# A GPS layer on one core: normed rows and queries issued earlier, 22 expert steps ahead, 60 posted columns, 21 diagonal tiles, statistics by algebra

## The chip, the cores and the metric

The kernel runs on one core of one Trainium2 chip. The metric is the device time of one execution in microseconds, as the median over runs. A core has five engines that run their own instruction streams and wait for each other by semaphores: TensorE (PE in the profile; its weight loads are shown as PEld), VectorE (DVE), ScalarE (ACT), GpSimd (POOL, which here issues all indirect DMAs) and SyncE (SP, which issues the plain DMAs).

## What is computed

`reference` is one layer of a graph network (GPS) over 3125 nodes with 256 features, in float32: a message-passing block and a linear-attention mixer on the normed nodes, added to the input, and then a mixture of experts with a graph-attention gate.

```
xn = _layernorm(x, axis=-1)
x = x + _L0_gnn_ref(xn, edge_attr_64, src, dst, ...) + _L0_mix_ref(xn[None], ...)[0]
x = x + _L0_ffn_ref(_layernorm(x, axis=-1)[None], ..., L0_ffn_edge_index)[0]
```

The message block gathers xn for 103125 edges sorted by target, appends 64 edge features, multiplies by a 320x256 matrix, sums by target, and runs a norm, a three-layer MLP with skips and a norm. The mixer has 4 layers. Each is

```
h = _layernorm(x, ln1_g[i], ln1_b[i])
x = x + _linear_attn(h, Wq[i], Wk[i], Wv[i], Wo[i], bo[i])
h = _layernorm(x, ln2_g[i], ln2_b[i])
x = x + (gelu(h @ W1[i] + b1[i], approximate=False) @ W2[i] + b2[i])
```

with 8 heads of 32. Queries are a softmax over the features of a head, keys a softmax over all nodes, and the context of a head is keys^T @ values. The expert block scores each node with graph attention over 65536 random edges (leaky_relu, softmax by target, sum of messages of 16 features), norms the scores, takes the best two of four experts, and adds their gated outputs; an expert is 256 to 512 to 256 with gelu.

## The kernel before

Nodes lie in 25 tiles of 128 rows (`NT`), kept in `xm` ([128, 25, 256]). `FOURS` are chunks of four tiles and a last one of one tile; `CHUNKS` is the same list with the one-tile chunk in sixth place, ahead of the last four tiles; `PAIRS` are chunks of two.

**Start.** `node_norm` takes bn_stats and bn_aggr of each tile, the root and reciprocal (`rstd_of`), and norms the rows on ACT in place. The normed rows go to `xn_d`. Then a flag (`unsorted`) is loaded into registers, which opens a branch for unsorted targets that is not taken. After it the statistics of the normed rows are taken again for the mixer (L330-331).

**Messages.** Edges are laid out 806 columns by 128. For each column POOL gathers 128 rows of `xn_d` (L515), in three rotating buffers `m_run` of 8 columns, and DVE adds a running sum over a partition's edges (L527), which is written to `run_d`. These sums are placed in DVE's order by a planner: every piece of the mixer calls `pace(us)`, which moves a clock and emits the columns that are due by it (one per 1.27 us). `beside(us)` spends idle time on a list of jobs that count, sort and place the 65536 gate edges.

**Mixer.** First the keys of layer 0 for all chunks. Then for each layer: `combined` makes `co` (the context with the output matrix), and each chunk goes through `attend` (add to `xm`, statistics), `normed_T` to `h2`, `ff_up` (8 blocks of matmuls and gelu), and `ff_down`. Behind it by one chunk run the next layer's `norm1` (in the middle of `ff_up`), `keys` (at its end; `query` is called at the end of `keys`) and `context` (after `ff_down`). The matmul outputs of `keys`, `query`, `attend`, `ff_up` and `ff_down` share three PSUM buffers named ps_a; a buffer is taken again once its last reader is done. In `keys` the two halves are both held until their exp, which needs the maximum over both (`top`).

**Placing the gate edges.** Jobs compute the sorted place of each edge. For 32 columns of 128 edges at a time (`SG`) the tile `place` is written by DVE (L691), and each column is then sent to `by_dst` by one indirect DMA on POOL (L856), except the first `SENT_BY_PE` = 3 of each group but the last: these are posted by a one-hot matmul on PE (`post`, L844-846) into one PSUM tile, which `sorted_edges` reads at the end. So 45 columns are posted and 467 sent. Message gathers and sends stand in one queue on POOL.

**Gate.** `finish` norms the final rows, writes a table of 24 features a node, and scatters the target's term to `tgt_d` on POOL (L917). Edges are then worked in 16 chunks of about 26 columns: POOL gathers 21 rows of the table for each (L1356), and 5 more are made by PE with a one-hot matrix (`which`, L1342, made from `low_of`, which `turned` transposes and writes through DRAM, L1329). Each `edge_chunk` runs scans on DVE and exps on ACT.

**Experts.** The experts' work is a generator of 164 steps (`expert`): a block of matmuls and a gelu, or the output of two tiles. `advance(n)` runs it up to step n. `LEAD` = 12 steps are issued ahead of the first edge chunk, 10 of them ahead of `turned`, and the rest is spread evenly over the chunks (`EACH`). The instructions of these steps are held in program order.

**End.** POOL gathers the sums of each node (L1594), DVE makes the gates, and the gated outputs are added: for the pairs in `by_pe` (8 pairs, 16 tiles) ACT scales an identity by each gate (L1730), PE multiplies it with the expert's output (L1732, summed over the four experts in PSUM), and DVE adds the sum (L1742); for the other 9 tiles DVE adds expert by expert (`by_turns`, L1750). Each pair is stored as it is done.

Of the kernel before, what the change touches and what calls it, by code (L numbers as in the profile page):

```python
# [13 lines left out]
ALU = mybir.AluOpType  # L14
# [45 lines left out]
def kernel(ctx: ExitStack, tc: tile.TileContext, a: dict, out: bass.AP):  # L60
# [47 lines left out]
    def stats(src, mv):  # L108
        st = small.tile([P, 6], F32, name="bst")
        V.bn_stats(st, src)  # L110
        V.bn_aggr(mv, st)
# [96 lines left out]
    def node_norm(c):  # L208
        for t in c:
            stats(xm[:, t, :], mv[:, t, :])  # L210
        r = rstd_of(mv[:, c[0]:c[-1] + 1, :], eps5)
        for i, t in enumerate(c):
            normed(xm[:, t, :], xm[:, t, :], r, i)
        nc.sync.dma_start(xn_d[c[0] * P:(c[-1] + 1) * P, :].rearrange("(c p) d -> p c d", p=P),
                          xm[:, c[0]:c[-1] + 1, :])

    for c in FOURS[:4]:
        node_norm(c)
# [108 lines left out]


    first_weights = layer_weights(0)
    for t in range(NT):  # L330
        stats(xm[:, t, :], mv[:, t, :])
    nc.sync.dma_start(res_d[:P, :].rearrange("p (a b) -> p a b", b=160), zero[:, :160].rearrange("p (o c) -> p o c", o=1).to_broadcast([P, 2, 160]))
    nc.sync.dma_start(run_d[NO_SUM:NO_SUM + 1, :].rearrange("p (a b) -> p a b", b=160),
                      zero[:1, :160].rearrange("p (o c) -> p o c", o=1).to_broadcast([1, 2, 160]))
# [483 lines left out]
    SG = 4 * GC  # L818
    number = [so.tile([P, SG], F32, name=f"number{i}") for i in range(2)]

    SENT_BY_PE, MID = 3, SRC // 2 - 486
    by_pe, posted = [], []

    def sent_by_pe(t):
# [220 lines left out]
        for kc in range(2):  # L1045
            V.scalar_tensor_tensor(wv[:, kc, :], ps[:, 1, :], -1.0 / D, wv[:, kc, :], op0=ALU.mult, op1=ALU.add)

    def normed_T(c, g, b, name):
        r = rstd_of(mv[:, c[0]:c[-1] + 1, :], eps5)
        hn = []  # L1050
        for i, t in enumerate(c):
            h = mw.tile([P, D], F32, name="hn", bufs=4)
            normed(h, xm[:, t, :], r, i)
            hn.append(h)
        hx = mw.tile([P, 2, 512], F32, name=name, bufs=1)
        transposed(hx[:, :, :len(c) * P], hn, g, b)
        return hx, r

    class Keys:
        pass  # L1060
# [9 lines left out]
    def halves(c):  # L1070
        return [c[i:i + 2] for i in range(0, len(c), 2)]

    def norm1(kv, l, c):
        kv.made[c[0]] = [normed_T(c, att_w[l]["g1"], att_w[l]["b1n"], "h1")]
        pace(1.5 * len(c) / 4)

    def keys(kv, l, c):

        (h1, r), = kv.made[c[0]]
        n = min((c[-1] + 1) * P, N) - c[0] * P  # L1080
        kT = mw.tile([P, 2, 512], F32, name="kT", bufs=1)
        if n < len(c) * P:
            V.memset(kT[:, :, n:len(c) * P], 0.0)
        here = small.tile([P, 2], F32, name="here", bufs=2)
        both = []
        for m in range(2):
            ps = pa.tile([P, 512], F32, name="ps_a")
            for kc in range(2):
                T.matmul(ps[:, :n], att_w[l]["wk"][:, kc, m * P:(m + 1) * P], h1[:, kc, :n], start=kc == 0, stop=kc == 1)  # L1089
            V.tensor_reduce(here[:, m:m + 1], ps[:, :n], AX.X, ALU.max)  # L1090
            both.append(ps)
        top = small.tile([P, 2], F32, name="top", bufs=2)
        down = small.tile([P, 2], F32, name="down", bufs=2)
        if kv.top is None:
            V.tensor_scalar_mul(top, here, -QS)
        else:
            V.scalar_tensor_tensor(top, here, -QS, kv.top, op0=ALU.mult, op1=ALU.min)
            V.tensor_tensor(down, top, kv.top, op=ALU.subtract)
        add = small.tile([P, 2], F32, name="add", bufs=2)
        for m in range(2):  # L1100
            S.activation(kT[:, m, :n], both[m][:, :n], AF.Exp, bias=top[:, m:m + 1], scale=QS, accum_out=add[:, m:m + 1])  # L1101
        if kv.top is None:
            V.tensor_copy(kv.ksum, add)
        else:
            S.activation(down, down, AF.Exp)
            V.tensor_tensor(kv.ksum, kv.ksum, down, op=ALU.mult)
            V.tensor_tensor(kv.ksum, kv.ksum, add, op=ALU.add)
        first = kv.top is None
        kv.top = top
        pace(3.7 * len(c) / 4)  # L1110
        qs_of = []
        for i0, ts in enumerate(halves(c)):
            qs_of.append(query(l, ts, h1, 2 * i0 * P))
        kv.made[c[0]] = [r, kT, down, first, qs_of]

    def query(l, c, h1, o):
        k = len(c)
        ps = pa.tile([P, 2, D], F32, name="ps_a")
        for i, t in enumerate(c):
            for kc in range(2):  # L1120
                T.matmul(ps[:, i, :], h1[:, kc, o + i * P:o + (i + 1) * P], att_w[l]["wq"][:, kc, :], start=kc == 0, stop=kc == 1)  # L1121
        q = mw.tile([P, 2 * HEADS, DH], F32, name="q", bufs=3)
        nh = k * HEADS
        ps_q = ps[:, :k, :].rearrange("p t (h d) -> p (t h) d", h=HEADS)
        qm = small.tile([P, 2 * HEADS, 1], F32, name="qm")
        V.tensor_reduce(qm[:, :nh, :], ps_q, AX.X, ALU.max)
        V.tensor_tensor(q[:, :nh, :], ps_q, qm[:, :nh, :].to_broadcast([P, nh, DH]), op=ALU.subtract)
        S.activation(q[:, :nh, :], q[:, :nh, :], AF.Exp, scale=QS)
        qs = small.tile([P, 2 * HEADS, 1], F32, name="qs")
        V.tensor_reduce(qs[:, :nh, :], q[:, :nh, :], AX.X, ALU.add)  # L1130
        V.reciprocal(qs[:, :nh, :], qs[:, :nh, :])
        V.tensor_tensor(q[:, :nh, :], q[:, :nh, :], qs[:, :nh, :].to_broadcast([P, nh, DH]), op=ALU.mult)
        pace(1.9 * k / 2)
        return q
# [104 lines left out]
    for l in range(DEPTH):  # L1239
        print('K',l,round(clock['now']),clock['columns'],len(jobs),clock['sent'],len(pieces))  # L1240
        if l == 0:
            fold(0)
        co = combined(kv, l)
        held[0] = GROUPS - 5
        beside(20.0)
        if l + 1 < DEPTH:
            att_w[l + 1] = layer_weights(l + 1)
        if l:
            ff_weights(l)
        if l == 1:  # L1250
            zero_fills()
        kv = keys_begin() if l + 1 < DEPTH else None
        attend(co, CHUNKS[0])
        h2, _ = normed_T(CHUNKS[0], ff_w[l]["g2"], ff_w[l]["b2n"], "h2")
        for j, c in enumerate(CHUNKS):
            last = CHUNKS[j - 1] if j else None
            ff_up(l, c, h2, 0, 3)
            if last and kv:
                norm1(kv, l + 1, last)
            ff_up(l, c, h2, 3, FF // P)  # L1260
            if last and kv:
                keys(kv, l + 1, last)
            if last and not kv:
                waiting.append(last)
                if j == len(CHUNKS) - 1:
                    while clock["columns"] < TM or pieces:
                        pace(2.0)
                        beside(3.0)
                for _ in range(2):
                    if len(waiting) > 1 and clock["columns"] == TM and not pieces:  # L1270
                        finish(waiting.pop(0))
            if j + 1 < len(CHUNKS):
                attend(co, CHUNKS[j + 1])
            ff_down(l, c)
            if j + 1 < len(CHUNKS):
                h2, _ = normed_T(CHUNKS[j + 1], ff_w[l]["g2"], ff_w[l]["b2n"], "h2")
            if last and kv:
                context(kv, last)
            if j == 1 and kv:
                fold(l + 1)  # L1280
        if kv:
            norm1(kv, l + 1, CHUNKS[-1])
            keys(kv, l + 1, CHUNKS[-1])
            context(kv, CHUNKS[-1])
        else:
            for c in waiting:
                finish(c)
# [216 lines left out]
        ("own_bin", "lo", "base"), ("own_bin", "hi", "base"), ("own_bin", "ohT1", "base"), ("own_bin", "ohT0", "base")))]  # L1504
    work = (w for e in range(NEXP) for w in expert(e))
    STEPS = NEXP * sum(FF2 // P + len(c[::2]) for c in FOURS)
    LEAD = 12
    EACH = (STEPS - LEAD) / N_FEW
    done, bound = [0], [False]

    def advance(to):
        while done[0] < min(to, STEPS) and next(work, False):
            done[0] += 1
# [6 lines left out]

    last, taken = None, gathered(0)
    many = nc.values_load(many_i[0:1, 0:1], min_val=0, max_val=1)
    advance(LEAD - 2)
    turned()
    marked(0)
    advance(LEAD)
    between(0, taken, LEAD)
# [211 lines left out]
            nc.sync.dma_start(out[c[0] * P:N, :], xm[:LAST, c[0], :])  # L1739

    def added(c, ps):
        V.tensor_tensor(xm[:, c[0]:c[-1] + 1, :], ps, xm[:, c[0]:c[-1] + 1, :], op=ALU.add)  # L1742
        stored(c)

    def by_turns(c):
# [4 lines left out]
                V.scalar_tensor_tensor(x, y, gate[:, t, e:e + 1], x, op0=ALU.mult, op1=ALU.add)  # L1750
        stored(c)

    by_pe, by_dve = PAIRS[:8], PAIRS[8:]
    for _ in gates(0):
        pass
    laid_out = []
# [1 line left out]
    for _ in gates(1):  # L1758
        for _ in range(1):
            if len(laid_out) < 3:  # L1760
                c = by_pe[len(laid_out)]
                laid_out.append((c, by_diagonals(c)))
    n_laid = len(laid_out)
    for k, c in enumerate(by_pe):
        added(*laid_out[k])
        if n_laid < len(by_pe):
            c = by_pe[n_laid]
            laid_out.append((c, by_diagonals(c)))
            n_laid += 1
        if k >= len(by_pe) - len(by_dve):  # L1770
            by_turns(by_dve[k - len(by_pe) + len(by_dve)])


# [22 lines left out]
```

## Time and profile before

| | us |
|---|---|
| median of 3 runs | 2413.49 (2407.11 to 2422.24) |
| profiled execution | 2414.89 |
| its span on the core | 2413.0 |
| first message gather on POOL | 34.56 |
| message gathers and layers 0, 1, most of 2 | until about 1207 |
| sends, rest of layer 2, layer 3 | 1207 to 1884 |
| scatters, table | 1884 to 1907 |
| 16 edge chunks and expert steps | 1907 to 2341 |
| node sums, gates, gated outputs | 2341 to 2413 |

The profile is one execution. Busy time counts an engine's own instructions; the idle time ahead of an instruction is given with what released it. For an indirect DMA on POOL the busy time is that of making the descriptors, and "issue" is time in which POOL waited for nothing that the profile shows. "L515" is a line of the kernel, and a line can be that of a helper: L110 and L111 are the two instructions of `stats`, L118 to L124 those of `rstd_of` and `normed`, L160 and L165 those of `transposed`. PEclk is the granted TensorE clock as a share of full speed.

### The profile page before, as it was taken

The page shows a single profiled execution, that of the slowest core. Times are in us where ns is not written, and L with a number is a line of the kernel's source. Part 1 is how long each engine was busy: PE and PEld are TensorE (multiplying, and loading weights), DVE is VectorE, ACT ScalarE, POOL GpSimd, SP SyncE. Part 2 cuts the span into 40 slices and gives each one's busy share as a digit, 9 for nine tenths or more (in the row PEclk, how much of TensorE's full clock was granted, in tenths as well). Part 3 has the DMA queues.
Part 4 walks back from the last instruction along what each step waited for, and adds up shares of the span by engine and source line. Part 5 has one row for each costly group of instructions (what it writes and reads, how often), then busy time and mean ns, then how long its engine had stood idle before and what let it go on. Part 6 is the DMA issues. An engine that isn't in the chain of part 4 may idle for free. (4 is left out here: it accounts for less than half of the span.)

```text
span 2413.0 us, 32637 instructions
## 1 busy us (share of the span) xinstructions
PE 2055.1 (85%) x10120; PEld 1420.4 (59%) x10120; DVE 1531.4 (63%) x4643; ACT 1101.1 (46%) x2028; POOL 1676.7 (69%) x1696
## 2 busy tenths in 40 slices
PE   3879787768799998799988888999989499999975
PEld 2656554555556666476666556676676265565544
DVE  7877876767647756576676475665662155655556
ACT  5734335535344453435456566656664033333324
POOL 4566767767666776567777767677777777777752
PEclk9989887888999999899988998999999699999987
DMA  8987887888866887668752232332320112211112
GB/s 252 327 277 255 272 249 258 230 231 275 255 214 223 265 249 235 222 218 254 251 159 58 52 96 68 93 81 70 80 50 5 23 31 44 54 29 31 25 20 62
DMA packets 318767, 370.50 MB, mean 154 GB/s; under 512 B 183707, under 2 KB 265732, under 8 KB 305380
## 3 DMA queue, kind: packets, MB, share of 16 engines
q1 hardware_dynamic: 251508, 253.66, 33.3%
q0 software_dynamic: 67072, 114.64, 18.0%
q8 instruction: 82, 1.34, 0.2%
q14 instruction: 105, 0.86, 0.1%
HBM read 207.95 MB, written 164.28 MB: 154 GB/s over the span
## 5 line engine op out<-in xcount | busy, mean ns | idle before, releaser
L515 POOL DMA_INDIRECT m_run<-xn_d,src_i x806 | 811.1, 1006 | 390.0 <-issue 216.7
L856 POOL DMA_INDIRECT by_dst<-pairs,place x467 | 465.7, 997 | 156.6 <-issue 136.6
L527 DVE SCALAR_TENSOR_TENSOR m_run<-m_run,stay 128x320 f32<-128x320 f32 x805 | 440.2, 547 | 63.7 <-DMA m_run<-xn_d,src_i 51.0
L1209 PE MATMUL ps_a<-h,w 128*128 128x512 f32 (+1 forms) x896 | 383.4, 568 | 4.4 <-ACT h L165 3.5
L1356 POOL DMA_INDIRECT rows_c<-tab_d,si x325 | 316.3, 973 | 98.9 <-issue 96.8
L1220 PE MATMUL ps_a<-w,gT 128*128 128x256 f32 x1600 | 367.6, 383 | 0.0
L1220 PEld LDWEIGHTS ps_a<-w,gT 128*128 128x128 f32 x1600 | 302.3, 191 | 50.5 <-issue 8.1
L1209 PEld LDWEIGHTS ps_a<-h,w 128*128 128x128 f32 x896 | 161.2, 200 | 148.6 <-issue 130.4
L1210 ACT ACTIVATE gT<-ps_a,b 128x512 f32<-128x512 f32 (+1 forms) x224 | 139.9, 633 | 147.3 <-PE ps_a L1209 145.8
L124 ACT ACTIVATE hn<-xm,rstd 128x256 f32<-128x256 f32 x225 | 120.7, 593 | 62.1 <-DVE rstd L120 59.6
L1121 PE MATMUL ps_a<-wq,h 128*128 128x256 f32 x400 | 104.2, 403 | 25.7 <-ACT kT L1101 16.6
L1477 ACT ACTIVATE hf<-ps_a,be 128x512 f32<-128x512 f32 (+1 forms) x112 | 70.3, 641 | 117.1 <-PE ps_a L1473 116.6
L1147 PE MATMUL ps_g<-xm,kr 128*128 128x256 f32 x400 | 111.8, 420 | 9.6 <-ACT kr L1145 9.3
L160 PE MATMUL ps_t<-ident,hn 128*128 128x128 f32 x450 | 81.2, 312 | 42.3 <-ACT hn L124 37.5
L792 ACT ACTIVATE earlier<-ps_t,slope 128x512 f16<-128x512 f32 x128 | 93.8, 775 | 49.2 <-PE ps_t L791 48.4
L1349 DVE SCALAR_TENSOR_TENSOR ps_g<-tile_ids,high_of,ps_g 128x500 f32<-128x500 f32 x50 | 37.1, 741 | 120.7 <-PE ps_g L1347 120.7
L1491 PE MATMUL ps_t<-we2h,hf 128*128 128x256 f32 x400 | 95.9, 392 | 14.2 <-ACT hf L1477 14.1
L1121 PEld LDWEIGHTS ps_a<-wq,h 128*128 128x128 f32 x400 | 76.4, 198 | 52.0 <-ACT kT L1101 22.7
L1147 PEld LDWEIGHTS ps_g<-xm,kr 128*128 128x128 f32 x400 | 80.7, 210 | 43.8 <-ACT kr L1145 28.3
L1089 PE MATMUL ps_a<-h,wk 128*128 128x512 f32 (+1 forms) x224 | 102.7, 592 | 3.3 <-ACT h L165 2.6
L110 DVE BATCH_NORM_STATS2 bst<-xm 128x6 f32<-128x256 f32 x250 | 97.5, 408 | 6.1 <-DVEq L303 4.1
L160 PEld LDWEIGHTS ps_t<-ident,hn 128*128 128x128 f32 x450 | 55.5, 154 | 73.7 <-ACT hn L124 55.4
(455 smaller groups left out, 3837.3 us busy)
## 6 DMA issues: line engine op xcount, KB each, us to landing
run_d<-m_run SPq DMA_DIRECT2D x100, 1280.0 KB
m_run<-in_edge_attr_dram SPq DMA_DIRECT2D x95, 256.0 KB
hr<-row_h SPq DMA_DIRECT2D x64, 256.0 KB
m_run<-xn_d,src_i POOLq DMA_INDIRECT x806
w<-in_L_mix_W_dram SPq DMA_DIRECT2D x8, 1024.0 KB
by_dst<-pairs,place POOLq DMA_INDIRECT x467
rows_c<-tab_d,si POOLq DMA_INDIRECT x325
run_d<-rows_c SPq DMA_DIRECT2D x15, 312.0 KB
```

What stands on the lines that cost most here:

```text
L124: S.activation(dst, src, AF.Identity, bias=r[:, 1, i:i + 1], scale=r[:, 0, i:i + 1])
L160: T.transpose(ps[:, i * P:(i + 1) * P], src[:, c * P:(c + 1) * P], ident)
L515: last_gather[0] = G.indirect_dma_start(out=m[:, t, :D], out_offset=None, in_=xn_d, in_offset=bass.IndirectOffsetOnAxis(ap=src_i[:, t0 + t ...
L527: add = V.scalar_tensor_tensor(m[:, t, :], before_m, stay[:, c:c + 1], m[:, t, :], op0=ALU.mult, op1=ALU.add)
L856: i = G.indirect_dma_start(out=by_dst, out_offset=bass.IndirectOffsetOnAxis(ap=place[:, t:t + 1], axis=0), in_=pairs0[:, t:t + 1], in_offs ...
L1089: T.matmul(ps[:, :n], att_w[l]["wk"][:, kc, m * P:(m + 1) * P], h1[:, kc, :n], start=kc == 0, stop=kc == 1)
L1121: T.matmul(ps[:, i, :], h1[:, kc, o + i * P:o + (i + 1) * P], att_w[l]["wq"][:, kc, :], start=kc == 0, stop=kc == 1)
L1147: T.matmul(ps_x[:, m, :], kr[:, m * P:(m + 1) * P], xm[:, t, :], start=i == 0 and m == 0, stop=i == len(c) - 1, skip_group_check=True)
L1209: T.matmul(ps[:, :w], ff_w[l]["w1"][:, kc, f * P:(f + 1) * P], h2[:, kc, :w], start=kc == 0, stop=kc == 1)
L1210: S.activation(gT[:, f, :w], ps[:, :w], AF.Gelu, bias=ff_w[l]["b1"][:, f:f + 1])
L1220: T.matmul(ps[:, i, :], gT[:, f, (2 * i0 + i) * P:(2 * i0 + i + 1) * P], ff_w[l]["w2"][:, f, :], start=False, stop=f == FF // P - 1, skip_ ...
L1356: G.indirect_dma_start(out=rows_c[:, t - COLS[j], :], out_offset=None, in_=tab_d, in_offset=bass.IndirectOffsetOnAxis(ap=si[:, t:t + 1], a ...
```

## The change

Six edits, all in the order and the amount of work; the arithmetic differs in one place.

- The statistics of the normed rows are not measured again. `node_norm` multiplies each variance twice by the reciprocal root and sets the mean to zero.
- `SENT_BY_PE` goes from 3 to 4: 60 columns are posted and 452 sent.
- `normed_T` is split into `normed_rows` (root, reciprocal, rows on ACT) and `columns_of` (transposes). The rows of `norm1` are made after 2 of the 8 blocks of `ff_up` and their transposes after 5 (before: both after 3). The rows for `h2` are made before `ff_down`, their transposes after it as before.
- `query` is called at the start of `keys`, ahead of the keys' matmuls.
- `LEAD` goes from 12 to 22: 14 steps, then `turned`, 6 more, `marked(0)`, 2 more.
- `by_pe` gets three more items (21 tiles), `by_dve` keeps two pairs (4 tiles), added after the seventh and eighth item of `by_pe`.

```diff
@@ node_norm
+        var, y = mv[:, c[0]:c[-1] + 1, 1], r[:, 0, :len(c)]
+        for _ in range(2):
+            V.tensor_tensor(var, var, y, op=ALU.mult)
+        V.memset(mv[:, c[0]:c[-1] + 1, 0], 0.0)
@@
-    for t in range(NT):
-        stats(xm[:, t, :], mv[:, t, :])
@@
-    SENT_BY_PE, MID = 3, SRC // 2 - 486
+    SENT_BY_PE, MID = 4, SRC // 2 - 486
@@
-    def normed_T(c, g, b, name):
+    def normed_rows(c):
         r = rstd_of(mv[:, c[0]:c[-1] + 1, :], eps5)
...
+        return r, hn
+
+    def columns_of(c, hn, g, b, name):
         hx = mw.tile([P, 2, 512], F32, name=name, bufs=1)
         transposed(hx[:, :, :len(c) * P], hn, g, b)
-        return hx, r
+        return hx
@@ keys
         (h1, r), = kv.made[c[0]]
+        qs_of = []
+        for i0, ts in enumerate(halves(c)):
+            qs_of.append(query(l, ts, h1, 2 * i0 * P))
...
         pace(3.7 * len(c) / 4)
-        qs_of = []
-        for i0, ts in enumerate(halves(c)):
-            qs_of.append(query(l, ts, h1, 2 * i0 * P))
@@ layer loop
-            ff_up(l, c, h2, 0, 3)
+            ff_up(l, c, h2, 0, 2)
+            rows_1 = normed_rows(last) if last and kv else None
+            ff_up(l, c, h2, 2, 5)
             if last and kv:
-                norm1(kv, l + 1, last)
-            ff_up(l, c, h2, 3, FF // P)
+                norm1(kv, l + 1, last, rows_1)
+            ff_up(l, c, h2, 5, FF // P)
...
                 attend(co, CHUNKS[j + 1])
+                rows_2 = normed_rows(CHUNKS[j + 1])[1]
             ff_down(l, c)
             if j + 1 < len(CHUNKS):
-                h2, _ = normed_T(CHUNKS[j + 1], ff_w[l]["g2"], ff_w[l]["b2n"], "h2")
+                h2 = columns_of(CHUNKS[j + 1], rows_2, ff_w[l]["g2"], ff_w[l]["b2n"], "h2")
@@
-    LEAD = 12
+    LEAD = 22
@@
+    advance(LEAD - 8)
+    turned()
     advance(LEAD - 2)
-    turned()
     marked(0)
     advance(LEAD)
@@
-    by_pe, by_dve = PAIRS[:8], PAIRS[8:]
+    by_pe, after_all, by_dve = PAIRS[:8], PAIRS[8:10] + PAIRS[12:], PAIRS[10:12]
...
+    by_pe = by_pe + after_all
     for k, c in enumerate(by_pe):
         added(*laid_out[k])
...
-        if k >= len(by_pe) - len(by_dve):
-            by_turns(by_dve[k - len(by_pe) + len(by_dve)])
+        if 6 <= k < 6 + len(by_dve):
+            by_turns(by_dve[k - 6])
```

## The prediction, made before the changed kernel was run

> **What bounds the kernel now.** I read the page first (busy shares, then the costliest groups), then busy time by stage, then the waits of PE and POOL, and last the timeline of single chunks and of the tail. The profiled run took 2414.89 us around a span of 2413.0, so 1.9 us lie outside the span; it stands 1.4 us above the median of 2413.49, which is within the spread of the three runs. Sums below are made in span time and added to the median.
>
> ```profile
> PE 2055.1 (85%) x10120; PEld 1420.4 (59%) x10120; DVE 1531.4 (63%) x4643; ACT 1101.1 (46%) x2028; POOL 1676.7 (69%) x1696
> ...
> L515 POOL DMA_INDIRECT m_run<-xn_d,src_i x806 | 811.1, 1006 | 390.0 <-issue 216.7
> L856 POOL DMA_INDIRECT by_dst<-pairs,place x467 | 465.7, 997 | 156.6 <-issue 136.6
> ```
>
> POOL looks only 69% busy, but each indirect DMA carries about 0.30 us of "issue" that is not counted: 1.26 us each. Some stages (start:end, length, then busy PE, PEld, DVE, ACT and POOL, then the granted clock):
>
> ```profile
> 490.00:830.00 340.00, 290.77 (x1270) 201.62 (x1269) 226.93 (x575) 141.84 (x247) 233.19 (x236) 0.91 0.77 247
> 830.00:1207.00 377.00, 345.89 (x1371) 237.32 (x1370) 246.05 (x597) 167.39 (x291) 259.94 (x265) 0.96 0.75 239
> 1207.00:1884.00 677.00, 601.73 (x4079) 439.20 (x4078) 397.65 (x1407) 389.21 (x700) 501.78 (x502) 0.93 0.28 72
> 1910.00:2322.00 412.00, 388.38 (x1294) 240.58 (x1294) 227.10 (x793) 134.53 (x204) 313.76 (x323) 0.97 0.19 34
> ```
>
> Layers 1 and 2 (650 to about 1330) are PE's: it is 92% busy in 830:1207, and a chunk of four tiles takes 47 us there, against 37 columns x 1.26 = 46.6 us on POOL. From 1207 to 1884 POOL (502 + 502x0.30 = 652 of 677 us) and PE share the bound; POOL runs dry whenever PE and DVE are late with `place`, once for 12.7 us at 1395. From 1910 to 2322 POOL is full (314 + 323x0.30 = 411 of 412 us); the rest is a serial tail.
>
> **Query ahead of keys (the largest part).** One chunk of layer 1 before:
>
> ```profile
> 716.98 3.60 PE L1089 MATMUL ps_a<-h,wk 128*128 128x512 f32 x8
> 720.41 3.96 PE L1121 MATMUL ps_a<-wq,h 128*128 128x256 f32 x16
> 724.21 3.62 PE L1198 MATMUL ps_a<-co,hT 128*128 128x256 f32 x16
> 728.97 0.39 PE L1217 MATMUL ps_a<-b_parts,ones_b 65*128 65x512 bf16 x1 [1.15 <-DVE q L1127]
> ```
>
> From keys to the first matmul of `ff_down`: 12.0 us, with one wait of 1.15. These blocks share three ps_a buffers. In the changed kernel's instruction order PE runs query half 0, query half 1, keys 0, keys 1, attend 0, attend 1. By then both keys tiles still hold their buffers: their exp needs `top`, which needs the maximum of both. So attend 1 takes the buffer of attend 0, and waits for the DVE add into xm. In DVE's order that add stands behind the maximum of keys 0, two sums, two reciprocals and two products of the query, three message columns (L527), the maximum of keys 1, and `top`. With this timeline's starts (128x512 on DVE 0.6 to 0.7 us, reciprocal 0.16, column 0.46; PE 1.98 us a query half, 1.8 for the others): keys 0 end at 5.8, maximum to 6.6, sums to 7.8, reciprocals to 8.1, products and three columns to 10.2, maximum and the last column to 11.4, `top` 11.5, add to 12.2. PE is done with attend 0 at 9.4, so it stands still **2.9 us**; `ff_down` starts at 14.1: +2.1 us. What is late next is everything on PE; nothing hides it, because PE is the bound here.
>
> A stop of 2.9 us may also cost clock. The Trainium skill ("TensorE: Matmul & The Clock Gate", section "What's actually happening") says the clock falls to half after an idle window of about 3.4 us; by that a stop of 2.9 us is free. The trace says otherwise (a stop of 2.98 us ends at 970.4; the seventh figure is the clock):
>
> ```profile
> 963.00:967.40 4.40, 4.05 (x20) 3.07 (x18) 3.16 (x10) 1.60 (x3) 3.46 (x4) 1.00 0.73 178
> 967.40:970.40 3.00, 0.04 (x1) 0.00 (x0) 2.93 (x12) 1.35 (x4) 2.11 (x3) 0.74 1.00 342
> 970.40:974.00 3.60, 2.92 (x9) 1.66 (x10) 0.41 (x1) 2.89 (x5) 2.69 (x4) 0.50 1.06 423
> 974.00:978.00 4.00, 4.00 (x6) 1.66 (x5) 0.69 (x1) 0.00 (x0) 3.08 (x4) 0.50 0.87 267
> ```
>
> Stops of 2.55 (at 1604), 2.75 (849), 2.98 and 3.37 us (1446) were each followed by 3.4 to 8 us at 0.50 to 0.59; stops of 2.00 and 2.45 us (1372, 1780) left it at 1.00. Half speed for 3.4 to 8 us costs 1.7 to 4 us. I take the row, 2.8 us in three of four stops: 2.1 a chunk. Sum: 5 chunks x 2 layers x (2.1 + 2.1) = **+42 us**; by the page's window, +21.
> In layer 0, where POOL or DVE set the pace up to 490, I take +3 (between +15 and -12: the wait of 9.3 us of query on the keys' exp at 512.87 may go). At the three layer ends both queries now stand ahead of the keys' chain to `co`: +2.7 less the waits of 1.4 and 1.3 that vanish, so 0 to +3 each: **+4**.
>
> **Normed rows earlier.**
>
> ```profile
> PE ps_t L160 <- ACT hn L124: 37.5, 11, 5.5
> PE ps_a L1121 <- ACT kT L1101: 16.6, 6, 9.3
> ```
>
> Of these waits, 5.3 us at 663 and 4.3 at 1005 are layer starts, which stay as they are. The ones taken away are those after the one-tile chunk, 4.92 us at 583 and 5.26 at 924: `ff_down` of one tile (3.5 us) is too short to cover the chain add, statistics, root, rows. Started before `ff_down`, the chain ends about 1 us after it, and the half clock after both stops (3.4 us each by the rows there) goes too: -2 x 7.5 = **-15 us**. Elsewhere the transposes did not wait, so 0. Of the activation tables 4 loads fewer are issued: 1.28 us each by the trace, 2.66 each with the drain by the skill ("ScalarE: Activation LUTs", "What ACT_TABLE_LOAD costs"); 5 or 11 us of an engine at 46%, so 0.
>
> **Statistics by algebra.** 25 pairs of bn_stats and bn_aggr go (25 x 0.39 = 9.8 us of DVE from 33.06 on), 21 small operations of 0.1 to 0.15 come (about 2.8). DVE reaches the flag some 1.6 us later than 28.98, since digit work is now scheduled ahead of it, so POOL's first gather (34.56) slips by that; PE's first layer matmuls come about 5 us earlier. POOL is not full at this point (120 us of gaps until 1207): **-5 us** (-8 to +2).
>
> **60 posted columns.** 15 sends leave POOL: 15 x 1.26 = 18.9 us. But:
>
> ```profile
> POOL by_dst L856 <- DVE place L691: 12.7, 1, 12.7
> ```
>
> POOL had nothing queued when `place` came at 1395, 1527, 1604 and 1720; what it saves before 1720 it waits at the next `place`. Only the 4 sends after that count: -5. The 15 posts add on PE 0.38 us each and wait 0.39 each (17.7 us over 45 for `post_hot`), on DVE 0.25 + 0.41: at most +11.6, of which I take half since PE is 89% busy. **+1 us** (-19 to +7).
>
> **22 steps ahead.** 10 steps of some 1.9 us move into PE's stops of 19.2 us (low_of, until 1889.84) and 15.4 (`which`, until 1916.54). Expert 1's five weight loads now enter SP's queue ahead of the low_d store. `which` is 17 us earlier than the first 21 gathers of rows_c, so a delay there is covered. Later POOL is the bound, so steps taken out of it give 0; one step fewer lies before the last chunk's exp: **-1 us**. A low_d store late by more than those 17 us would cost.
>
> **21 diagonal tiles.** In the tail:
>
> ```profile
> 2388.27 11.78 ACT L1730 ACTIVATE diag<-ident,gate 128x128 f32<-128x128 f32 x40
> ...
> 2407.41 0.68 DVE L1742 TENSOR_TENSOR xm<-ps_a,xm 128x512 f32<-128x512 f32 x1
> ```
>
> DVE's 36 turns fall to 16 (20 x 0.39 = 8 us less), ACT's copies rise from 64 to 84 (0.295 each, ends 2406.0). But PE takes 8 matmuls x 0.216 = 1.73 us a tile without a break from 2388.7 to 2406.1: five more tiles end at 2414.7, the last add at 2415.1 instead of 2408.1: **+7 us**.
>
> Sum: 42 + 3 + 4 - 15 - 5 + 1 - 1 + 7 = +36: **2449 us**.
>
> **Rivals.**
> 1. The stop comes, the clock stays (chance 0.20): 36 - 21 = +15, 2428. For it: the page's window, and two stops near 2.4 us left no mark.
> 2. Not slower: POOL and not PE decides (0.18). Place: 1207 to 1884. If POOL keeps a backlog at each `place`, PE's stops are absorbed and all 15 sends count: -18.9 - 5 - 1 + 7 = -18, 2395; with PE's late sum kept below POOL's saving of 19 us. Against it: the empty queue at four places, and 92% PE ahead of them. With the 9.3 us of layer 0 also gone it falls below 2389.
> 3. Worse (0.12): every stop halves the clock, also four in layer 0 (+15 more), and the columns come late into DVE's row: +60, 2473.
>
> Likeliest 0.50: 2449, itself 2435 to 2465. A measurement here tells about 1% (24 us). Faster by over 1%: half of rival 2, 0.09, so 0.10 with the rest. Slower (over 2438): 0.44 of the likeliest, 0.12, and 0.04 of rival 1: 0.60; same 0.30. Range 2393 to 2474, which leaves out the far ends of rivals 2 and 3.
>
> **What would show it.** A wait of attend (`co,hT`) on DVE xm of some 3 us in each chunk, with half clock after it; the hn waits at 583 and 924 gone; POOL waiting longer for `place`; PE's diagonals ending 8 us after ACT's. Wrong if attend 1 does not wait, or if layers 1 and 2 take no longer than before.

## The result, and the profile after

The changed kernel takes 2430.96 us (median of 6 runs, 2427.71 to 2435.57), the kernel before 2414.86 in the same series: a ratio of 1.0062, with a 95% interval of 1.0044 to 1.0080. So it is slower, by some 15 us or 0.6%, where the forecast said 36. The profiled execution has a span of 2429.2 us.

The waits of PE in the changed kernel (total, times, longest):

```profile
PE ps_a L1204 <- DVE xm L1205: 31.6, 10, 6.7
...
PE ps_t L160 <- ACT hn L124: 19.4, 7, 5.0
PE ps_t L1149 <- ACT kT L1110: 18.6, 7, 5.1
...
PE ps_a L1098 <- DVE q L1133: 15.3, 6, 10.1
```

The first line is new: `attend` waits for the add into xm. The second was 37.5 us before. One chunk of layer 1 shows where (the timeline of PE, then part of DVE's):

```profile
710.40 3.62 PE L1127 MATMUL ps_a<-wq,h 128*128 128x256 f32 x16
713.85 3.60 PE L1098 MATMUL ps_a<-h,wk 128*128 128x512 f32 x8
717.28 1.89 PE L1204 MATMUL ps_a<-co,hT 128*128 128x256 f32 x8
721.88 3.10 PE L1204 MATMUL ps_a<-co,hT 128*128 128x256 f32 x8 [2.70 <-DVE xm L1205]
724.78 0.63 PE L1223 MATMUL ps_a<-b_parts,ones_b 65*128 65x512 bf16 x1
```

```profile
715.77 0.69 DVE L1099 TENSOR_REDUCE here<-ps_a 128x1 f32<-128x512 f32 x1 [0.30 <-PE ps_a L1098]
716.38 1.27 DVE L1136 TENSOR_REDUCE qs<-q 128x16 f32<-128x512 f32 x2
717.56 0.37 DVE L1137 RECIPROCAL qs<-qs 128x16 f32<-128x16 f32 x2
717.85 0.68 DVE L1138 TENSOR_TENSOR q<-q,qs 128x512 f32<-128x512 f32 x1
718.45 0.55 DVE L529 SCALAR_TENSOR_TENSOR m_run<-m_run,stay 128x320 f32<-128x320 f32 x1
718.91 0.72 DVE L1138 TENSOR_TENSOR q<-q,qs 128x512 f32<-128x512 f32 x1
719.55 0.54 DVE L529 SCALAR_TENSOR_TENSOR m_run<-m_run,stay 128x320 f32<-128x320 f32 x1
720.01 0.68 DVE L1099 TENSOR_REDUCE here<-ps_a 128x1 f32<-128x512 f32 x1
720.61 0.54 DVE L529 SCALAR_TENSOR_TENSOR m_run<-m_run,stay 128x320 f32<-128x320 f32 x1
721.07 0.16 DVE L1104 TENSOR_SCALAR top<-here 128x2 f32<-128x2 f32 x1
721.14 0.68 DVE L1205 TENSOR_TENSOR xm<-ps_a,xm 128x512 f32<-128x512 f32 x1
```

PE is done with attend 0 at 719.2 and stands until 721.88: 2.70 us, where the forecast had 2.9. The row of DVE work ahead of the add is the one that was predicted, down to the third column between the second maximum and `top`. `ff_down` starts 14.4 us after the first matmul of the block (before 12.0). The forecast had 14.1 without any loss of clock; here 1.1 us of the 14.4 is clock, since the second attend half takes 3.10 us and not 1.99. In the next chunk, which keeps its clock, the block takes 13.3 us (763.76 to 777.04). The windows after this stop, after the next one, and after a third (start:end, length, busy PE, PEld, DVE, ACT, POOL, then the clock):

```profile
721.88:725.28 3.40, 3.40 (x10) 2.55 (x11) 2.30 (x8) 2.12 (x5) 2.48 (x4) 0.61 0.36 107
725.28:728.68 3.40, 3.40 (x16) 2.92 (x15) 3.37 (x12) 0.30 (x1) 0.82 (x1) 0.89 0.68 261
775.21:778.61 3.40, 3.40 (x16) 2.91 (x17) 3.33 (x12) 2.20 (x6) 2.49 (x4) 1.00 0.38 112
824.13:827.53 3.40, 3.40 (x10) 2.60 (x11) 2.68 (x10) 2.21 (x6) 2.18 (x3) 0.63 0.93 333
```

After 721.88 the loss is 0.39 + 0.11 of 3.40 us = 1.7 us, one such window at half clock, and after 775.21, at the same length of stop (2.67 us), it is nothing. Of eight such stops between 565 and 1176, six show half clock and two do not. Of the ten chunks in layers 1 and 2, seven stop ahead of attend 1; the two ahead of a one-tile chunk, which has no attend 1, stop ahead of `ff_down` instead; one shows no such stop. The two ahead of `ff_down` keep their clock, though one is the longest stop of the nine:

```profile
874.50 0.38 PE L1223 MATMUL ps_a<-b_parts,ones_b 65*128 65x512 bf16 x1 [3.31 <-DVE xm L1205]
```

```profile
874.50:877.90 3.40, 3.40 (x16) 3.00 (x16) 2.67 (x10) 2.77 (x7) 2.79 (x3) 1.00 0.39 116
```

So five of nine stops in layers 1 and 2 cost a window.

How far the changed kernel stands behind at a few places (start of the instruction before and after, in us):

| | before | after | shift |
|---|---|---|---|
| first message gather | 34.56 | 33.5 | -1.1 |
| layer 1, first transposes of `h2` | 663.05 | 658.00 | -5.1 |
| layer 2, the same | 1005.66 | 1008.42 | +2.8 |
| layer 2, sixth start of `ff_down` (one tile) | 1305.33 | 1324.90 | +19.6 |
| layer 2, seventh | 1374.20 | 1384.97 | +10.8 |
| last `place` | 1791.8 | 1801.7 | +9.9 |
| last send | 1883.1 | 1895.9 | +12.8 |
| last gather of rows_c | 2321.7 | 2335.8 | +14.1 |
| first gather of sums | 2341.8 | 2350.9 | +9.1 |
| last add | 2407.4 | 2424.0 | +16.6 |

Layers 1 and 2 up to the sixth chunk lose 25 us, some 9 come back in one chunk, 5 come back ahead of the sums, 7.5 go in the tail. POOL, from 1207 to 1910:

```profile
POOL by_dst L858 <- DVE place L693: 29.1, 3, 19.3
POOL aggr L601 <- PE ps_t L617: 12.2, 2, 11.9
```

It waited 12.7 and 4.8 us in these two lines before: what 15 sends less took off POOL (18.9 us) it spends waiting for `place` and the node sums, 24 us more. The tail (PE, then ACT):

```profile
2418.57 1.46 PE L1742 MATMUL ps_a<-y_all,diag 128*128 128x256 f32 x6
...
2422.03 1.46 PE L1742 MATMUL ps_a<-y_all,diag 128*128 128x256 f32 x6
2423.32 0.59 PE L1742 MATMUL ps_a<-hT,diag 128*128 128x256 f32 x2
```

```profile
2415.32 1.28 ACT L1740 ACTIVATE diag<-ident,gate 128x128 f32<-128x128 f32 x4 [0.45 <-PE ps_a L1742]
```

PE works two tiles every 3.46 us to the end, and ACT itself waits 0.45 us a tile for PE to free a buffer, as PE is the slower of the two.

### The profile page after: what moved, and what is told of

It reads as the page before. It is cut to its first block, busy times and chain, and to the rows that moved or that the text cites. A ratio compares the mean times of both kernels' runs of the same rounds, so it can differ in the third digit from the quotient of the medians.

```text
span 2429.2 us, 32710 instructions
## 1 busy us (share of the span) xinstructions
PE 2095.3 (86%) x10175; PEld 1451.8 (60%) x10175; DVE 1525.5 (63%) x4627; ACT 1102.2 (45%) x2044; POOL 1657.2 (68%) x1681
## 5 line engine op out<-in xcount | busy, mean ns | idle before, releaser
L858 POOL DMA_INDIRECT by_dst<-pairs,place x452 | 450.8, 997 | 167.9 <-issue 133.3
L1215 PE MATMUL ps_a<-h,w 128*128 128x512 f32 (+1 forms) x896 | 388.5, 575 | 4.7 <-ACT h L165 3.4
L1204 PE MATMUL ps_a<-co,hT 128*128 128x256 f32 x400 | 112.1, 425 | 33.4 <-DVE xm L1205 31.6
L1204 PEld LDWEIGHTS ps_a<-co,hT 128*128 128x128 f32 x400 | 80.8, 210 | 58.9 <-DVE xm L1205 35.5
L1098 PE MATMUL ps_a<-h,wk 128*128 128x512 f32 (+1 forms) x224 | 97.6, 572 | 15.3 <-DVE q L1133 15.3
L1500 PE MATMUL ps_t<-we,hf 128*128 128x256 f32 x400 | 97.8, 398 | 14.9 <-ACT hf L1486 14.9
L1500 PEld LDWEIGHTS ps_t<-we,hf 128*128 128x128 f32 x400 | 79.3, 200 | 33.6 <-ACT hf L1486 16.4
```

Of the source, the lines that this page charges most:

```text
L858: i = G.indirect_dma_start(out=by_dst, out_offset=bass.IndirectOffsetOnAxis(ap=place[:, t:t + 1], axis=0), in_=pairs0[:, t:t + 1], in_offs ...
L1204: T.matmul(ps[:, i, :], hT[:, m, t * P:(t + 1) * P], co[:, m, :], start=m == 0, stop=m == 1)
L1215: T.matmul(ps[:, :w], ff_w[l]["w1"][:, kc, f * P:(f + 1) * P], h2[:, kc, :w], start=kc == 0, stop=kc == 1)
L1500: T.matmul(ps[:, i, :], hh[f][:, (i0 + i) * P:(i0 + i + 1) * P], we2[f], start=False, stop=f == FF2 // P - 1, skip_group_check=True)
```

## The experiments

**The theories.** S: the loss comes from the query's place, through the stop ahead of attend 1 and the clock behind it. O: the stops only stand where other waits stood, and the loss comes from the posted columns and the tail. A measured ratio is to the kernel before on the same chip, with its 95% interval; 0.001 is 2.4 us.

**Query after the keys, all else changed (q_back_b).**

```diff
         (h1, r), = kv.made[c[0]]
-        qs_of = []
-        for i0, ts in enumerate(halves(c)):
-            qs_of.append(query(l, ts, h1, 2 * i0 * P))
...
         pace(3.7 * len(c) / 4)
+        qs_of = []
+        for i0, ts in enumerate(halves(c)):
+            qs_of.append(query(l, ts, h1, 2 * i0 * P))
```

> 

> Once more the changed kernel with query after the keys' exp, since in the first try the kernel before itself took 3532 us, with engines idle for 20 to 30 us at a time with no wait of the program behind it, so that its size says nothing of 20 us. Theory S: 20 us below the changed kernel, 2408 to 2414, so level with or just under the kernel before. Rival O: within 5 us of the changed kernel.

Measured: 2398.81 us, ratio 0.9932 (0.9914 to 0.9950). That is 0.0130 or 31 us below the changed kernel, more than theory S said. The other five parts together make the kernel 16 us faster (forecast: -15 - 5 + 1 - 1 + 7 = -13). The same chunk in this kernel:

```profile
708.17 3.60 PE L1095 MATMUL ps_a<-h,wk 128*128 128x512 f32 x8
711.61 3.96 PE L1127 MATMUL ps_a<-wq,h 128*128 128x256 f32 x16
715.40 3.62 PE L1204 MATMUL ps_a<-co,hT 128*128 128x256 f32 x16
720.16 0.39 PE L1223 MATMUL ps_a<-b_parts,ones_b 65*128 65x512 bf16 x1 [1.15 <-DVE q L1133]
```

The stop is gone and the 12.0 us are back. Chunk by chunk, the changed kernel is 2.2 us behind this one at the first `ff_down` of layer 1 (679.96 against 677.74) and 33.4 behind at the last start of `ff_down` in layer 2 (1384.97 against 1351.56): nearly all of the price lies in layers 1 and 2. O falls. Between these two places, in the changed kernel and then in this one:

```profile
679.96:1384.97 705.01, 634.12 (x2875) 445.65 (x2874) 452.84 (x1167) 328.52 (x585) 483.23 (x492) 0.94 0.63 200
```

```profile
677.74:1351.56 673.82, 622.87 (x2874) 435.58 (x2873) 447.69 (x1167) 327.98 (x585) 479.45 (x486) 0.96 0.65 209
```

The same matmuls keep PE busy 11.3 us longer, at a lower clock, and PE stands 19.9 us longer (70.9 against 51.0). So of 31.2 us about 11 are clock and 20 are standing.

**Query first, nothing else (q_alone_b).** The same move in the kernel before.

> 

> Once more the kernel before with query first in keys and nothing else. Theory S: +20 us on the kernel before, ratio 1.006 to 1.011. Rival O: within 5 us, ratio 0.998 to 1.002.

Measured: 2454.18 us, ratio 1.0161 (1.0143 to 1.0179): +39 us, twice what was expected here. The stops are the same (2.67 us at 731.5, 785.1, 834.0, 926.1, 1140.2, and 2.71 to 3.50 at the rest). So the part costs 31 us beside the others and 39 by itself. The clock's share is larger here: from the first `ff_down` of layer 1 to the last of layer 2 PE is busy 646.4 us against 628.4 in the kernel before, 18 us, and stands 15.5 us longer.

**The stop filled (filled).**

```diff
+            if busy and ts[0] == c[0]:
+                idle = pt.tile([P, 512], F32, name="ps_t")
+                for _ in range(2):
+                    T.matmul(idle, co[:, 0, :P], co.rearrange("p a d -> p (a d)"), start=True, stop=True)
```

> 

> The changed kernel with two matmuls more between attend 0 and attend 1, into a buffer that nobody reads (they leave the result as it is): about 1.8 us of the stop of 2.7 us is filled, so no idle stretch of over 1 us is left for the clock. If the half clock after the stops is part of the price (six of ten stops, 1.7 us each): -10 us, 2421, and 1.00 after each stop. If only the stop itself costs: 2431, or a little more.

Measured: 2425.53 us, ratio 1.0053 (1.0036 to 1.0069). By the ratios that is 0.0009 or 2 us below the changed kernel (5 us by the medians), less than the intervals can tell. The trace is clearer (PE, then the window behind the stop):

```profile
717.12 1.89 PE L1204 MATMUL ps_a<-co,hT 128*128 128x256 f32 x8
718.85 1.88 PE L1209 MATMUL ps_t<-co 128*128 128x512 f32 x4
721.68 1.99 PE L1204 MATMUL ps_a<-co,hT 128*128 128x256 f32 x8 [0.95 <-DVE xm L1205]
723.51 0.38 PE L1227 MATMUL ps_a<-b_parts,ones_b 65*128 65x512 bf16 x1
```

```profile
723.00:727.00 4.00, 4.00 (x21) 3.41 (x20) 3.96 (x11) 1.12 (x2) 3.09 (x4) 1.00 0.61 223
```

Attend 1 starts as late as in the changed kernel (721.68), but takes 1.99 us and not 3.10, at a clock of 1.00. The first transposes of `h2` of layer 2 start at 1001.73 against 1008.42, and the span is 2422.7 against 2429.2. So the filler wins back about 7 us in the profiled executions, and 2 us, within noise, by the ratios; the rows of the changed kernel give 10 us (six stops at 1.7, one of them in layer 0), and PE's busy time above gives 11. By none of these does the clock cost the 21 us of the forecast.

**Keys' exp by halves, query still first (top_halves).** Each half has its own `top` and exp right after its maximum, so that the buffer of keys 0 is free early.

```diff
             V.tensor_reduce(here[:, m:m + 1], ps[:, :n], AX.X, ALU.max)
-            both.append(ps)
-        if kv.top is None:
-            V.tensor_scalar_mul(top, here, -QS)
-        else:
-            V.scalar_tensor_tensor(top, here, -QS, kv.top, op0=ALU.mult, op1=ALU.min)
...
-        for m in range(2):
-            S.activation(kT[:, m, :n], both[m][:, :n], AF.Exp, bias=top[:, m:m + 1], ...)
+            if kv.top is None:
+                V.tensor_scalar_mul(top[:, m:m + 1], here[:, m:m + 1], -QS)
+            else:
+                V.scalar_tensor_tensor(top[:, m:m + 1], here[:, m:m + 1], -QS, kv.top[:, m:m + 1], op0=ALU.mult, op1=ALU.min)
+            S.activation(kT[:, m, :n], ps[:, :n], AF.Exp, bias=top[:, m:m + 1], ...)
```

> 

> The changed kernel, query still first, with the keys' maximum, top and exp made half by half, so that the buffer of keys 0 is free before attend 1 asks for it. Theory S: the stop is the whole price of the query's place: -25 to -32 us, 2399 to 2406, and no wait of attend on the add into xm. Rival: the price is DVE's longer row of work ahead of the keys' exp, and the stop moves on to ff_down: within 8 us of the changed kernel.

Measured: 2410.20 us, ratio 0.9991 (0.9978 to 1.0003): 0.0071 or 17 us below the changed kernel. Between the two expectations, for a reason that the trace shows:

```profile
715.22 1.89 PE L1202 MATMUL ps_a<-co,hT 128*128 128x256 f32 x8
718.92 1.99 PE L1202 MATMUL ps_a<-co,hT 128*128 128x256 f32 x8 [1.81 <-ACT kT L1106]
```

Attend 1 no longer waits for the add but for the exp of keys 0, which DVE's query work still holds up: the stop is 1.81 us, not nothing. The clock stays at 1.00 behind all six stops of 1.81 to 1.82 us in layers 1 and 2, and also behind the one of 2.72 us at 865.86.

**16 diagonal tiles (diag_back_b, and with query after the keys: best).**

```diff
-    by_pe, after_all, by_dve = PAIRS[:8], PAIRS[8:10] + PAIRS[12:], PAIRS[10:12]
+    by_pe, by_dve = PAIRS[:8], PAIRS[8:]
```

> 

> Once more the changed kernel with 16 diagonal tiles, since the first try lay in a disturbed run. If PE's diagonal matmuls set the end of the tail: -7 to -8 us, 2423. If gates and stores set it: 2431.

> 

> The changed kernel with both costly parts undone: query after the keys' exp, and 16 diagonal tiles. If the two prices add up: 2399 - 7.5 = 2391, ratio 0.990 to the kernel before. If the tail's gain is lost in the store behind it: 2399.

Measured: 2426.10 us, ratio 1.0042 (1.0025 to 1.0060) for the first, 0.0020 or 5 us below the changed kernel; 2388.03 us, ratio 0.9905 (0.9880 to 0.9931) for the second, 0.0027 or 6.5 us below q_back_b. In both comparisons the two intervals overlap, so neither alone shows a gain; but it is twice the same sign, and near the 7 us of the forecast. As far as these intervals tell, the prices add up.

**The other parts, each alone on the kernel before.**

> 

> Once more the kernel before with the normed rows made earlier, and nothing else. By the prediction's term: -15 us, ratio 0.994. By the trace of the changed kernel (the waits after the one-tile chunk fall to about 2 us, and the clock still halves after them): -6 us, ratio 0.9975.

Measured: 2400.97 us, ratio 0.9924 (0.9904 to 0.9944): -18 us. Not for the reason given. The waits after the one-tile chunk are still there:

```profile
PE ps_t L160 <- ACT hn L124: 27.5, 9, 5.3
```

At 583 and 918 they last 4.55 and 4.1 us (before 4.92 and 5.26). The gain lies in other places. One is the fifth chunk of layer 1, 4.2 us: a wait of 2.75 us for the scaled keys (L1147 on ACT kr at 849) is gone. The larger one is the last of layer 2, from its one-tile `ff_down` to the next. Kernel before, then rows_alone_b:

```profile
1305.30:1374.20 68.90, 57.39 (x323) 37.71 (x322) 34.73 (x118) 46.27 (x84) 52.74 (x54) 0.90 0.28 72
```

```profile
1302.60:1361.90 59.30, 52.58 (x325) 35.47 (x324) 33.13 (x117) 43.62 (x83) 45.34 (x46) 0.98 0.32 84
```

Some 320 matmuls take 57.4 us at a clock of 0.90 and 52.6 at 0.98, and PE's idle time falls from 11.5 to 6.7 us: 9.6 us in one stretch, half of it in slower matmuls. It is no accident of one execution: this stretch takes 68.9 to 73.6 us in the four kernels without this part that ran undisturbed (before, q_alone_b, stats_alone, post_alone) and 58.4 to 61.0 in the eight with it.

> 

> The kernel before with the statistics by algebra alone. By the prediction's term: -5 us, ratio 0.998 (0.9967 to 1.001). If the earlier start is kept through the layers, since the changed kernel stood 5 to 8 us ahead of the kernel before up to the start of layer 1: -8 us, ratio 0.9967. If POOL's column gathers eat it: 1.000.

Measured: 2413.89 us, ratio 0.9991 (0.9979 to 1.0003): -2 us, not told from nothing.

> 

> The kernel before with 60 posted columns alone. By the prediction's term the saved sends are waited away at the next place: +1 us (-5 to +7), ratio 1.000. Rival, POOL decides the stage from 1207 to 1884: -19 us, ratio 0.992.

Measured: 2407.28 us, ratio 0.9964 (0.9948 to 0.9980): -9 us, between the two. The profiled execution is the slowest of its 13 (2416.42) and shows no gain: POOL's wait for `place` grows from 12.7 to 22.8 us, and that for the node sums (`aggr`) from 4.8 to 10.0. What the others gained, no trace shows.

**Both repaired (best_top_q).** Query after the keys, 16 diagonals, and the keys' exp by halves.

> 

> The changed kernel with query after the keys, 16 diagonal tiles, and the keys' exp by halves. If early release of the keys' buffers also helps the old order (query's second half waited for it): -3 to -6 us against the same kernel without it, ratio 0.988. If that order had no wait on them that counts: 0.9905.

Measured: 2376.23 us, ratio 0.9829 (0.9807 to 0.9851), 0.0076 or 18 us below the same kernel with the exp in one: it beats both kernels, and by more than either expectation. The chunk:

```profile
702.89 3.60 PE L1097 MATMUL ps_a<-h,wk 128*128 128x512 f32 x8
706.32 3.62 PE L1125 MATMUL ps_a<-wq,h 128*128 128x256 f32 x16
709.77 3.62 PE L1202 MATMUL ps_a<-co,hT 128*128 128x256 f32 x16
713.23 0.38 PE L1221 MATMUL ps_a<-b_parts,ones_b 65*128 65x512 bf16 x1
```

From keys to `ff_down` it takes 10.3 us without one wait, against 12.0 before and 14.4 in the changed kernel. Short holds, which the list of waits hardly shows, added up: the query took 3.96 us for 3.62 of work, and PE stood 1.15 us before `ff_down`.

**Runs on a disturbed chip.** On three chips the kernel before itself took 3532, 3547 and 3545 us. In the trace of q_back there ACT and DVE stand idle for over 20 us at a time with no instruction of the program as the releaser, so these runs say nothing of microseconds. Their ratios to the kernel before: q_back 0.9933 (0.9905 to 0.9960), q_alone 1.0180 (1.0127 to 1.0233), diag_back 1.0033 (1.0003 to 1.0063), rows_alone 0.9881 (0.9827 to 0.9935), the same signs as above. The steps ahead were only run there:

> 

> The kernel before with 22 steps ahead and turned after 14, nothing else. By the prediction's term: -1 us, ratio 1.000. By the changed kernel's trace, where the stretch from the last row gather to the first sum gather is 5 us shorter: -5 us, ratio 0.998.

> 

> Once more, since in the try before this one the kernel before itself took 3547 us. By the prediction's term: -1 us, ratio 1.000; by the changed kernel's trace: -5 us, ratio 0.998.

Measured: 1.0005 (0.9980 to 1.0030) and 0.9994 (0.9972 to 1.0017). This does not tell 0 and -5 us apart, so their own price stays open.

## Why the prediction was wrong

The direction and the mechanism of the largest part were right; its size was not. The forecast had 49 us for that part and the runs show 31 beside the others, and these 18 us are most of the gap between +36 and +15. The other five parts came to -16 us together, forecast -13, though singly some were right for a wrong reason.

| part | forecast, us | alone, us | beside the others, us |
|---|---|---|---|
| query ahead of keys (42 + 3 + 4) | +49 | +39 | +31 |
| normed rows | -15 | -18 | |
| statistics | -5 | -2 | |
| posted columns | +1 | -9 | |
| steps ahead | -1 | open | -5 in the trace |
| diagonals | +7 | | +5 and +6.5 |
| sum | +36 | | measured +15 |

**The term that failed is the clock of the query's part.** "I take the row, 2.8 us in three of four stops: 2.1 a chunk", 21 us in all. The changed kernel shows 7 to 11 us: five of nine stops in layers 1 and 2 at 1.7 us each, 0.9 a chunk, and 11 us in PE's busy time with the layer end between them. That is 10 to 14 of the 18 us; the rest is spread over the part's other terms. Both factors were too high, the price more than the frequency. The price came from stops followed by half clock for up to 8 us, while these cost one stretch of 3.4 us. The trace before held a closer case, the stop of 2.75 us at 849:

```profile
849.48:852.88 3.40, 3.40 (x8) 2.71 (x9) 0.00 (x0) 2.77 (x4) 2.55 (x3) 0.51 0.62 164
852.88:856.28 3.40, 3.40 (x19) 2.48 (x18) 0.77 (x2) 2.29 (x5) 2.73 (x3) 1.00 0.36 105
```

Here PE has work without a gap behind the stop, as it has behind attend 1, and the loss is one window, 1.7 us. Behind the other three stops that the forecast took, PE stands again for 0.5 to 1.1 us in the first window (2.92 us busy of 3.60 after 970.4). That these gaps make the half clock last is likely, but no run tests it. By itself the part cost 18 us in PE's busy time (q_alone_b), so the clock's price also hangs on the kernel around it.

The Trainium skill's idle window ("TensorE: Matmul & The Clock Gate", section "What's actually happening"), taken as a limit for one stop, would have said 0. That is not right either: 2.67 us is shorter than the 3.4 us that it names, and the clock fell. Rival 1, the same stop at full clock, gave 2428 and came within 3 us of the result, by luck: the clock did fall, and a smaller loss by standing and the other parts made up for it.

**The stop itself** was worked out to 2.9 us and measured 2.70. Its effect on PE's schedule, +2.1 us in each of ten chunks, was 21 us; PE stood 19.9 us longer over layers 1 and 2, about 17.5 of it in the chunks and the rest at the layer end. This was a term without a row of its own, built from the order of instructions and the durations of others, and it nearly held.

**The normed rows** had the right size by a wrong reason. The waits "taken away" after the one-tile chunk lost 0.4 and 1.2 us of five when the part was alone, and 3 us each in the changed kernel; the gain came from places in which the forecast had priced nothing ("Elsewhere the transposes did not wait, so 0"). That the size came out is luck. The four activation table loads fewer did come (150 to 146); a switch takes 1.30 us in the trace before (gelu ends at 2318.07, exp starts at 2319.38), so of the two figures the smaller one fits.

**The posted columns** were priced as if every saved send were waited away, from an empty queue at four places. The trace before shows that at two only: POOL waits 12.7 us at 1395, and 4.8 and 2.1 around 1525, while at 1604 and 1720 no gap is longer than the 0.30 us that every send has. In the changed kernel the 24 us of new waits bear the term out. Alone the part still gave -9 us, so a part of the saved sends is not waited away, and where is not shown.

**The steps ahead** were priced at -1 us, one step fewer before the last chunk's exp. In the traces the stretch from the last row gather to the first sum gather fell from 20.1 to 15.1 us; it is 14.4 to 15.4 in every undisturbed kernel with 22 steps and 19.7 to 20.2 in every one with 12. The step that fell away there is one of two tiles, 3.7 us of PE's time.

**Statistics and diagonals** came within 3 us of the forecast, the statistics with a measured gain that is not told from nothing.

The terms measured alone sum to +10 us with the steps at -5 (39 - 18 - 2 - 9 - 5 + 5), +2 with the query's price beside the others, against +15 (11 to 19). Each has an interval of about 4 us, so the sum does not show whether the parts act on each other.

## What to carry to other kernels

Moving independent work ahead of a chain is not free when both pass through the same few buffers and the same in-order engine: write down which buffer each block will take, and what stands ahead of the instruction that frees it. Here an earlier release, one more small DVE instruction a chunk, which lets each half of the keys go as soon as it can, was worth 17 us with the query first and 18 with the query last. And a price for lost clock has to be taken from a stop with the same work around it, not only of the same length. Such a loss can stand where no long wait is listed: from 1305 to 1374 of the kernel before the clock is 0.90, and no wait there is over 2.0 us.

## What the runs showed of the hardware

In this kernel the length of a stop alone does not tell whether TensorE's clock falls. In the changed kernel six of eight stops of 2.67 to 3.20 us ahead of attend 1 were followed by one stretch near 3.4 us at half clock, while the stops of 3.31 us at 874.50 and 2.82 us at 1226.01 kept 1.00. A stop of 3.32 us at the same place in q_alone_b was followed by 0.59 for 6.8 us. In top_halves six stops of 1.81 to 1.82 us never cost clock, but in the changed kernel one of 1.74 us, with a shorter wait 3 us ahead of it, did:

```profile
1381.36 1.22 PE L641 MATMUL ps_a<-gh,gw 128*128 128x256 f32 x2 [1.74 <-ACT gh L165]
```

```profile
1381.36:1384.80 3.44, 3.44 (x9) 2.62 (x10) 0.93 (x4) 1.54 (x7) 2.53 (x4) 0.50 0.02 0
```

What decides, no run here shows. A filler of two matmuls inside the stop kept the clock at 1.00.
